# LayerNorm's sums and output projection in one pass over y, with counts from Relu, image statistics first, and fewer scan steps beside norm 0

## The chip, the core and the metric

The kernel runs on one core of one Trainium2 chip. The metric is the device time of one execution in microseconds (us), as the median of several executions. The core has TensorE (matmuls), VectorE, ScalarE and GpSimd, and a SyncE queue from which this kernel issues nearly all its transfers (DMA). Each engine works through its own instructions in order and waits for other engines and transfers by semaphores. In the profile they are PE, DVE, ACT, POOL and SP; PEld is the loading of weights into TensorE, and SPq an entry of SyncE's DMA queue.

## What is computed

Four images of 96 channels and 128x128 pixels go through two layers. The first is a state-space block on 192 channels; the second splits the result by its sign and runs an attention with 3x3 convolutions. Cut to what matters here (the group norms before each layer, weights and biases are left out; `layer_norm` stands for a mean and variance over the whole image):

```python
# layer 0, per image
z  = silu(depthwise_conv3x3(in_w @ gn(x)))               # 192 channels
for k in range(4):                                       # rows, columns, and both reversed
    h[l] = exp(delta[l] * A) * h[l-1] + delta[l] * B[l] * u[l]     # the scan, u = z in order k
    y_k  = C * h + D * u
ym = y0 + y1 + y2 + y3
yn = (ym - mean_c(ym)) * rsqrt(var_c(ym) + 1e-5) * ln_w + ln_b     # over the 192 channels of a pixel
x  = x + out_w @ yn                                      # 192 -> 96 channels

# layer 1, per image
v   = gn(x) - mean(gn(x))
x1, x2 = relu(v), v - relu(v)
pos = count(v > 0)                                       # with the sums of x1 and x1**2, both halves' statistics
x1, x2 = x1 + normed(x1), x2 + normed(x2)                # "the halves"
# attention: two convolved maps of x1 and x2 give a softmax weight per channel pair and tap,
# a third map of x1 is convolved with it; a fourth, of x2, is multiplied by x1
out = x + residual + w_full @ concat(layer_norm(attention), layer_norm(conv(x2)) * x1)
```

The scan runs over 16384 positions; the kernel cuts it into 384 steps of 1024 positions on 128 channels.

## The kernel before

The kernel is written as Python generators that emit instructions and yield a cost. `co_run(left, right, pace)` interleaves two of them: for each unit of cost that `left` has emitted, `right` emits `pace` units. `Later` holds back a function for some ticks, so that it is emitted behind other work. The emission order is then the order of each engine up to the end of image 0's maps.

The body before the loop over images, cut:

```python
last = ssm_scan(zb, xdt, xbc, yms, ready)
with tc.tile_pool(name="wp", bufs=1, side="left") as wp:
    weights = project_weights(wp)
    stats = {}
    stats[0], run = image_stats(0, wp)
    with tc.tile_pool(name="a0", bufs=4, side="left") as p2:
        drain(run(p2, 4))
    first = len(traced())
    for images, pace in (([0], 0.25), ([1], 0.75), ([2, 3], 1.35)):
        left = projections(images, weights, stats, wp, psl)
        co_run(left, last, pace)                 # input projection beside the scan
        drain(left)
four, nine = pair_weights()
...
left = imgs[0].norm(yms[0][0], psl, "left")      # "norm 0": ssm_output, then split_norm
co_run(left, last, 1.2)
drain(left)
left = direct_maps(imgs[0], psl)                 # "the maps of image 0", nine-tap convolutions
co_run(left, last, 0.75)
drain(left)
drain(last)                                      # what is left of the scan
in_order(first)
...
for b in range(NB):                              # attention of image b
    light = []
    if b:
        light.append(imgs[b - 1].close(psr, "right"))
    if b + 1 < NB:
        imgs[b + 1] = Image(b + 1)
        light.append(imgs[b + 1].norm(yms[(b + 1) // 2][(b + 1) % 2], psr, "right"))
    light = chain(*light)
    left = imgs[b].attend(psl)
    co_run(left, light, 0.5 if b else 1.5)
    drain(left)
    drain(light)
```

Image 0's maps are made ahead of the loop, so its attention there is short, and "norm 1" runs beside it.

A half of a scan step on VectorE, ScalarE and TensorE, cut:

```python
nc.tensor.matmul(pBC, lhsT=wbc[...], rhs=xr[...])        # B and C spread over channels; three banks
nc.vector.tensor_mul(p, dl, p)                           # times B
nc.vector.tensor_tensor_scan(h, h, p, init, ALU.mult, ALU.add)
nc.vector.tensor_mul(dl, dA, pC)                         # times C
# besides: softplus and exp on ScalarE, times u and the sum into y on GpSimd
```

`ssm_output`, which makes the LayerNorm and the output projection of an image in two passes over y (SN = 1024 positions, NS = 16 chunks), cut:

```python
mq = [p2.tile([128, H], F32, name=f"mq{i}", bufs=1) for i in range(2)]
ahead = load_y(0)
for c in range(NS):                                  # pass 1
    y = ahead
    if c + 1 < NS:
        ahead = load_y(c + 1)
    sq = p2.tile([C, 2, SN], F32, name="rx")
    nc.scalar.activation(sq, y, AF.Square)
    ... # 8 matmuls with mean192: means of y and y*y; copied to st, and by DMA into mq's rows
ahead = load_y(0)
later.flush()
m, q = mq
nc.vector.tensor_mul(m, m, m)                        # the whole image at once, 128 x 128
nc.vector.tensor_sub(q, q, m)
nc.vector.tensor_scalar(q, q, 0.0, None, ALU.max)
nc.scalar.activation(q, q, AF.Sqrt, bias=eps)
nc.vector.reciprocal(q, q)
rd = dram.tile([L], F32, name="rd")
nc.sync.dma_start(rd.rearrange("(p f) -> p f", f=W), q)
...
for c in range(NS):                                  # pass 2
    y, (rb, xc) = ahead, near
    if c + 1 < NS:
        ahead, near = load_y(c + 1), load_r(c + 1)   # load_r: rd spread over 96 partitions, and x
    t = p2.tile([C, SN], F32, name="xo")
    for h in range(2):
        ... # 2 matmuls po = outws.T @ y
        # held back: t = po * rb; t = t + outbs + xc; bn_stats(t); then the store to xnew
```

The counting loop of `split_norm` (the loop for the halves behind it isn't changed):

```python
for i in range(NS):
    y = ahead
    if i + 1 < NS:
        ahead = piece(i + 1)
    z = p2.tile([C, SN], F32, name="xz")
    nc.scalar.activation(z, y, AF.Identity, scale=a, bias=shift0)
    later(lambda ...: nc.vector.tensor_scalar(
        y, z, 0.0, None, ALU.is_gt, ALU.add, accum_out=cnt[:, 0, i : i + 1]))
    r = p2.tile([C, SN], F32, name="xr")
    nc.scalar.activation(r, z, AF.Relu, accum_out=cnt[:, 1, i : i + 1])
    nc.scalar.activation(r, r, AF.Square, accum_out=cnt[:, 2, i : i + 1])
```

Of the kernel before, what the change touches and what calls it, by code (L numbers as in the profile page):

```python
# [60 lines left out]
def kernel(  # L61
# [150 lines left out]

    wdt = const.tile([KS, 3, NK, 128], BF16, name="wdt", tag="wdt")
    wbc = const.tile([KS, 3, 2, 128], BF16, name="wbc", tag="wbc")
    with tc.tile_pool(name="w0", bufs=1) as w0:
        wf = w0.tile([RANK, NK, 2 * C], F32, name="wf")
        nc.gpsimd.dma_start(wf, dt_wT)
        one = w0.tile([3, 128], BF16, name="one")  # L220
        nc.vector.memset(one, 1.0)
        nc.vector.memset(wdt, 0.0)
        nc.vector.memset(wbc, 0.0)
        flat = "p k c -> p (k c)"
        pieces = split3(w0, wf.rearrange(flat), [RANK, NK * 2 * C])
        for img, ch, g, p, n in PARTS:
            row = img * KI if g == 1 else 0
            for w in range(3):
                src = pieces[w].rearrange("p (k c) -> p k c", k=NK)[:, :, ch : ch + n]
                for i in range(3):  # L230
                    at = row + w * 18 + i * RANK
                    nc.gpsimd.dma_start(wdt[at : at + RANK, g, :, p : p + n], src)
            for q in range(2):
                at = row + 54 + q
                nc.gpsimd.dma_start(wbc[at : at + 5 : 2, g, q, p : p + n], one[:, :n])

    outws = const.tile([C, 2, C], F32, name="outws", tag="outws")
    outbs = const.tile([C, 1], F32, name="outbs", tag="outbs")
    with (
        tc.tile_pool(name="w3", bufs=1) as w3,  # L240
        tc.tile_pool(name="ps0", bufs=1, space=PSUM) as ps0,
    ):
        outw = w3.tile([C, 2, C], F32, name="outw")
        nc.sync.dma_start(outw, out_wT)
        for j in range(2):
            nc.vector.tensor_scalar(
                outws[:, j], outw[:, j], lnw[:, j : j + 1], None, ALU.mult
            )
        pb = ps0.tile([C, 1], F32, name="pb")
        for j in range(2):  # L250
            nc.tensor.matmul(
                pb, lhsT=outw[:, j], rhs=lnb[:, j : j + 1], start=(j == 0), stop=(j == 1)
            )
        nc.vector.tensor_add(outbs, pb, outb)

        pw = ps0.tile([C, C], F32, name="pw")
        for j in range(2):
            nc.tensor.matmul(
                pw, lhsT=mean192, rhs=outws[:, j], start=(j == 0), stop=(j == 1)
            )  # L260
        nc.vector.tensor_sub(outws, outws, pw.unsqueeze(1).to_broadcast([C, 2, C]))
# [635 lines left out]
    def ssm_output(b, yms, xnew, stats, ps, side):  # L897

        with tc.tile_pool(name="c2", bufs=2, side=side) as p2:
            xb = x[b].rearrange("c h w -> c (h w)")
            ym = yms.rearrange("(j p) l -> p j l", j=2)
            later = Later()

            def load_y(c):
                y = p2.tile([C, 2, SN], F32, name="y")
                nc.sync.dma_start(y, ym[:, :, bass.ts(c, SN)])
                return y

            mq = [p2.tile([128, H], F32, name=f"mq{i}", bufs=1) for i in range(2)]
            ahead = load_y(0)
            for c in range(NS):
                y = ahead
                if c + 1 < NS:
                    ahead = load_y(c + 1)
                sq = p2.tile([C, 2, SN], F32, name="rx")
                nc.scalar.activation(sq, y, AF.Square)
                later.tick()
# [981 lines left out]
```

## Time and profile before

| | before |
|---|---|
| median of 3 runs | 7268.67 us (7267.92 to 7278.59) |
| span of the profiled run | 7274.5 us |
| TensorE busy | 5881.5 us, 81% |
| VectorE busy | 4795.2 us, 66% |
| GpSimd busy | 3343.3 us, 46% |
| ScalarE busy | 3086.6 us, 42% |
| moved by DMA | 1277.65 MB, 176 GB/s |
| mean granted TensorE clock | 0.88 |

The shares are averages over stages that differ. The landmarks of the stages are these: the first matmul of the input projection stands at 104.5 us and the last at 2217.7 us; the first square of norm 0 at 2292.2 us; the maps of image 0 begin at 2900.1 us; the last scan on VectorE is at 3672.6 us, and the last maps matmul at 3770.3 us; the matmuls of attention 1 begin at 4284.4 us.

In the lines of the profile, `L977 PE MATMUL bank<-y,outws` is an instruction of line 977 that writes the tile `bank` from `y` and `outws`. A view by stretches gives start and end, the length, and for each engine the busy time and, in brackets, the number of instructions; then the granted clock as a share of full speed, the busy share of the 16 DMA engines and what they moved.

### The profile page before, as it was taken

To read this page: it belongs to the slowest core of one execution; us is meant where nothing else is said; L and a number is where in the kernel's file an instruction comes from. 1 tells how busy PE (TensorE), PEld (TensorE's weight loads), DVE (VectorE), ACT (ScalarE), POOL (GpSimd) and SP (SyncE) were. 2 spreads that over 40 slices of the span, in tenths; PEclk is the share of its full clock that TensorE was granted. 3 is DMA by queue.
4 is the path that set the end of the run, shared out by engine and by line. 5 is a ranking of instruction groups with operands and counts; after the bars stand their busy time and mean duration, and the time that the engine had idled before them with its cause. 6 is when DMAs were issued, how large, how long until landed. Compare 5 with 4: busy or idle time off the path is not lost. (4 is left out here: it accounts for less than half of the span.)

```text
span 7274.5 us, 72922 instructions
## 1 busy us (share of the span) xinstructions
PE 5881.5 (81%) x22236; PEld 2380.6 (33%) x22236; DVE 4795.2 (66%) x6658; ACT 3086.6 (42%) x3734; POOL 3343.3 (46%) x2050
## 2 busy tenths in 40 slices
PE   4989978788996743899987658997889987798977
PEld 1323322222221110444442224343334343334432
DVE  2247768788895778566625667366775457776587
ACT  1347767677774466455521342305223115122102
POOL 2026657778794355557611234233443333444541
PEclk9999989988996555999988879998899998899998
DMA  4556666666766765555557766686666777665455
GB/s 116 141 142 183 185 186 182 190 188 172 208 181 165 224 168 177 160 168 154 165 142 200 203 202 182 165 216 171 208 184 169 181 196 198 200 178 145 117 149 166
DMA packets 768475, 1277.65 MB, mean 176 GB/s; under 512 B 198562, under 2 KB 507710, under 8 KB 755604
## 3 DMA queue, kind: packets, MB, share of 16 engines
q1 hardware_dynamic: 765892, 1272.71, 63.6%
q8 instruction: 179, 2.93, 0.2%
q14 instruction: 212, 1.74, 0.1%
q0 software_dynamic: 2192, 0.27, 0.1%
HBM read 908.45 MB, written 296.46 MB: 166 GB/s over the span
## 5 line engine op out<-in xcount | busy, mean ns | idle before, releaser
L1219 POOL TENSOR_TENSOR t<-y 128x768 f32<-128x768 f32 (+1 forms) x352 | 543.0, 1543 | 1957.9 <-DMA y<-vd 577.1
L597 PE MATMUL bank<-y,wp 128*128 128x512 f32 (+3 forms) x3584 | 1326.5, 627 | 70.5 <-DMA y<-y 36.6
L795 POOL TENSOR_TENSOR dl<-dl,u 128x1024 f32<-128x1024 f32 x384 | 1018.1, 2651 | 760.2 <-ACT dA L763 478.2
L828 POOL TENSOR_TENSOR y<-y,dl 128x1024 f32<-128x1024 f32 x384 | 1051.8, 2739 | 666.8 <-DVE dl L820 635.4
L1243 PE MATMUL bank<-t,wd 128*128 128x384 f32 (+2 forms) x4224 | 1158.9, 500 | 57.9 <-DVE ring L1286 20.3
L816 DVE TENSOR_TENSOR_SCAN dA<-dA,pBC 128x512 f32<-128x512 f32 x768 | 981.5, 1278 | 30.7
L1292 ACT COPY s<-bank 128x384 f32<-128x384 f32 (+2 forms) x292 | 135.9, 465 | 1871.9 <-PE bank L1254 1778.6
L820 DVE TENSOR_TENSOR dl<-dA,pBC 128x512 f32<-128x512 f32 x768 | 528.3, 688 | 508.6 <-PE pBC L772 453.0
L772 PE MATMUL pBC<-xr,wbc 60*128 60x512 bf16 (+1 forms) x1536 | 547.6, 418 | 372.3 <-DVE dA L816 318.6
L1243 PEld LDWEIGHTS bank<-t,wd 128*128 128x128 f32 (+1 forms) x4224 | 559.9, 170 | 611.3 <-issue 324.4
L1243 PE MATMUL bank<-t,wa 128*96 128x384 f32 (+1 forms) x1408 | 561.8, 548 | 235.8 <-DVE t L1220 123.2
L597 PEld LDWEIGHTS bank<-y,wp 128*128 128x128 f32 (+3 forms) x3584 | 461.4, 170 | 765.3 <-issue 678.8
L1601 PE MATMUL bank<-y,wn 128*128 128x384 f32 (+5 forms) x2408 | 653.8, 502 | 37.1 <-DMA y<-x1d 26.1
L639 ACT ACTIVATE dl<-pd,dtb 128x512 f32<-128x512 f32 x768 | 486.2, 684 | 248.1 <-PE pd L746 224.3
L1284 DVE TENSOR_TENSOR d<-s,bank 128x384 f32<-128x384 f32 (+2 forms) x292 | 156.1, 534 | 574.8 <-ACT s L1292 465.5
L799 DVE TENSOR_TENSOR pBC<-dl,pBC 128x512 f32<-128x512 f32 x768 | 527.0, 686 | 1.1
L763 ACT ACTIVATE dA<-dl,negA 128x1024 f32<-128x1024 f32 x384 | 420.2, 1141 | 2.3
L1243 PEld LDWEIGHTS bank<-t,wa 128*96 128x96 f32 x1408 | 240.7, 185 | 547.5 <-issue 407.9
L1601 PEld LDWEIGHTS bank<-y,wn 128*128 128x128 f32 (+3 forms) x2408 | 308.0, 167 | 321.6 <-issue 166.5
L639 ACT ACT_TABLE_LOAD x240 | 307.9, 1283 | 237.0 <-PE pd L746 234.0
L772 PEld LDWEIGHTS <-wbc 60*128 60x128 bf16 (+1 forms) x1536 | 113.1, 99 | 872.6 <-issue 862.1
L1220 POOL TENSOR_TENSOR t<-y 128x384 f32<-128x384 f32 (+1 forms) x352 | 368.3, 1046 | 0.0
(247 smaller groups left out, 7888.5 us busy)
## 6 DMA issues: line engine op xcount, KB each, us to landing
u<-zb SPq DMA_DIRECT2D x192, 1024.0 KB
y<-yms SPq DMA_DIRECT2D x128, 768.0 KB
xr<-xdt SPq DMA_DIRECT2D x768, 72.0 KB
yms<-y SPq DMA_DIRECT2D x96, 512.0 KB
xn<-xnew SPq DMA_DIRECT2D x128, 384.0 KB
y<-y SPq DMA_DIRECT2D x128, 258.2 KB
zb<-z SPq DMA_DIRECT2D x64, 512.0 KB
y<-vd SPq DMA_DIRECT2D x168, 193.8 KB
```

Of the source, the lines that this page charges most:

```text
L597: nc.tensor.matmul(blocks(pz[p:e]), lhsT=ws[k][:, d, c : c + e - p], rhs=window(ys[k], at, d, n), start=(i == 0), stop=(i == len(terms) - 1),)
L639: nc.scalar.activation(dst, src, AF.Softplus, bias=bias)
L763: nc.scalar.activation(live[m]["dA"], live[m]["dl"], AF.Exp, scale=negA[:, g % 3, k : k + 1])
L772: nc.tensor.matmul(p, lhsT=wbc[0 : xr.shape[0], steps[n][0] % 3, q], rhs=xr[:, at : at + CH], start=True, stop=True,)
L795: nc.gpsimd.tensor_mul(t, t, u_view(n))
L799: nc.vector.tensor_mul(p, live[n]["dl"][:, bass.ts(half, CH)], p)
L816: nc.vector.tensor_tensor_scan(h, h, p, init, ALU.mult, ALU.add)
L820: nc.vector.tensor_mul(live[n]["dl"][:, sl], live[n]["dA"][:, sl], live[n]["C", half])
L828: nc.gpsimd.tensor_add(v, v, t.rearrange("p (a b) -> p a b", b=W))
L1219: eng.tensor_sub(v[:, 0:2], of(y, 0), of(y, 2))
L1243: nc.tensor.matmul(pc[p:e, :n], lhsT=w[:, i, c : c + e - p], rhs=t[k][:, i, :n], start=(k == 0), stop=False,)
L1601: nc.tensor.matmul(pc[p:e, :n].rearrange("p (h w) -> p h w", w=W), lhsT=w[:, c : c + e - p], rhs=v[:, :, 0:W], start=(i == 0), stop=(i == ...
```

## The change

1. **One pass over y.** A chunk's squares, sums, reciprocal root, projection, scaling and store follow each other, a chunk behind. y is loaded once and the result is written over y's first half. The root is made for each chunk (8 x 128) and goes through DRAM to 96 partitions chunk by chunk. y has three buffers, the squares one.
2. **Counts from Relu.** Relu with scale and bias reads the loaded piece itself, so the Identity pass is left out; the count is taken from Relu's result, which is over 0 where the value is.
3. **Image statistics load first.** The statistics of image 0 are emitted ahead of the weights of the projection, the scan and the output, which are wrapped into functions.
4. **Paces.** The scan's pace beside norm 0 goes from 1.2 to 0.25, and beside the maps of image 0 from 0.75 to 0.95.

The aim is to read y once, to take ScalarE's third pass away, to begin the projection sooner, and to place the scan's steps beside the maps rather than beside norm 0.

```diff
@@ ssm_output (cut)
-            mq = [p2.tile([128, H], F32, name=f"mq{i}", bufs=1) for i in range(2)]
-            ahead = load_y(0)
-            for c in range(NS):
...
+            def deviations(c):
+                y = ys[c]
+                sq = p2.tile([C, 2, SN], F32, name="sq", bufs=1)
+                st = p2.tile([128, CH], F32, name="st", bufs=1)
+                mq = p2.tile([RS, 2, W], F32, name="mq")
+                m, q = mq[:, 0], mq[:, 1]
+                pm = bank(ps)
+                def sums():
...                 # the 8 matmuls as before
+                    later(lambda: nc.scalar.copy(st, pm))
+                    later(rows, 1)
+                def rows():
+                    for i in range(2):
+                        nc.sync.dma_start(mq[:, i], st[32 * i : 32 * i + 65 : 64])
+                    later(inverse, 1)
+                def inverse():
+                    nc.vector.tensor_mul(m, m, m)
+                    nc.vector.tensor_sub(q, q, m)
+                    nc.vector.tensor_scalar(q, q, 0.0, None, ALU.max)
+                    nc.scalar.activation(q, q, AF.Sqrt, bias=eps[0:RS])
+                    nc.vector.reciprocal(q, q)
+                    later(back)
+                def back():
+                    to = rd[bass.ts(c, SN)]
+                    nc.sync.dma_start(to.rearrange("(p f) -> p f", f=W), q)
+                    near[c] = p2.tile([C, 2, SN], F32, name="rx")
+                    nc.sync.dma_start(near[c][:, 1], xb[:, bass.ts(c, SN)])
+                    later(lambda: nc.sync.dma_start(near[c][:, 0], to.partition_broadcast(C)))
+                nc.scalar.activation(sq, y, AF.Square)
+                later(sums, 1)
+            load_y(0)
+            load_y(1)
+            yield 2.0
+            for c in range(NS + 1):
+                if c < NS:
+                    deviations(c)
+                later.tick()
+                yield 1.4
+                later.tick()
+                yield 1.4
+                if c:
+                    y = ys.pop(c - 1)
+                    rx = near.pop(c - 1)
+                    t = y[:, 0]
+                for h in range(2):
+                    if c:
...                     # 2 matmuls po = outws.T @ y of chunk c - 1
...                     # scaled(): t = po * rx[:, 0]; t = t + outbs + rx[:, 1]; bn_stats(t)
+                        later(scaled, 1)
+                        if h:
+                            to = xnew[:, bass.ts(c - 1, SN)]
+                            later(lambda t=t, to=to: nc.sync.dma_start(to, t), 2)
+                    later.tick()
+                    yield 1.4
+                later.tick()
+                yield 1.4
+                later.tick()
+                load_y(c + 2)
+                yield 1.4
@@ split_norm, counting loop
+                r = p2.tile([C, SN], F32, name="xr")
+                nc.scalar.activation(
+                    r, y, AF.Relu, scale=a, bias=shift0, accum_out=cnt[:, 1, i : i + 1]
+                )
+                later(lambda y=y, r=r, i=i: nc.vector.tensor_scalar(
+                    y, r, 0.0, None, ALU.is_gt, ALU.add, accum_out=cnt[:, 0, i : i + 1]
+                ))
                 z = p2.tile([C, SN], F32, name="xz")
-                nc.scalar.activation(z, y, AF.Identity, scale=a, bias=shift0)
...
-                r = p2.tile([C, SN], F32, name="xr")
-                nc.scalar.activation(r, z, AF.Relu, accum_out=cnt[:, 1, i : i + 1])
-                nc.scalar.activation(r, r, AF.Square, accum_out=cnt[:, 2, i : i + 1])
+                nc.scalar.activation(z, r, AF.Square, accum_out=cnt[:, 2, i : i + 1])
                 later.tick()
-                yield 3.5
+                yield 2.4
@@ the body
-        weights = project_weights(wp)
         stats = {}
         stats[0], run = image_stats(0, wp)
         with tc.tile_pool(name="a0", bufs=4, side="left") as p2:
             drain(run(p2, 4))
+        weights = project_weights(wp)
+        wdt, wbc = scan_weights()
+        outws, outbs = output_weights()
...
-    co_run(left, last, 1.2)
+    co_run(left, last, 0.25)
     drain(left)
     left = direct_maps(imgs[0], psl)
-    co_run(left, last, 0.75)
+    co_run(left, last, 0.95)
```

## The prediction

> **What bounds the kernel now.** I read first the busy time of each engine by stretch, with the cuts at the kernel's stages; then TensorE's order of instructions, to count the scan steps in each stage; last the timelines of the DMA queue and VectorE around norm 0, because single transfers decide there. The average (TensorE busy 81%) says little: the stages have different limits.
>
> The stretches of the kernel before (start:end, length, busy us of each engine with its instruction count, granted clock, DMA share, GB/s):
>
> ```profile
> core 0: us, PE busy (x) PEld busy (x) DVE busy (x) ACT busy (x) POOL busy (x), PEclk, DMA share, GB/s
> 0.00:105.00 105.00, 3.02 (x13) 2.65 (x14) 31.65 (x78) 6.82 (x8) 41.72 (x76) 1.00 0.37 95
> ...
> 2218.00:2290.00 72.00, 19.22 (x64) 4.67 (x62) 38.82 (x48) 20.12 (x24) 32.81 (x13) 0.55 0.50 131
> 2290.00:2400.00 110.00, 93.71 (x300) 16.32 (x301) 34.96 (x43) 63.46 (x60) 30.43 (x13) 0.55 0.77 208
> 2400.00:2625.00 225.00, 146.34 (x237) 42.77 (x237) 182.07 (x209) 88.05 (x95) 90.94 (x37) 0.62 0.77 215
> 2625.00:2740.00 115.00, 44.93 (x90) 10.32 (x91) 90.75 (x133) 104.42 (x135) 73.06 (x30) 0.50 0.54 155
> 2740.00:2900.00 160.00, 41.51 (x78) 8.33 (x77) 149.23 (x143) 109.30 (x107) 97.20 (x60) 0.50 0.56 182
> 2900.00:3675.00 775.00, 732.85 (x3011) 350.67 (x3011) 503.07 (x620) 405.87 (x537) 459.49 (x176) 0.96 0.57 162
> 3675.00:3770.00 95.00, 94.35 (x433) 54.00 (x432) 8.59 (x17) 18.72 (x35) 2.14 (x1) 1.00 0.45 110
> 3770.00:3900.00 130.00, 91.50 (x383) 26.63 (x380) 42.65 (x76) 38.58 (x38) 20.50 (x18) 0.78 0.66 165
> 3900.00:4085.00 185.00, 131.43 (x327) 51.14 (x324) 122.47 (x193) 5.97 (x11) 33.53 (x23) 0.82 0.87 234
> 4085.00:4180.00 95.00, 62.91 (x157) 23.21 (x156) 61.56 (x129) 57.09 (x88) 23.94 (x25) 0.77 0.65 175
> 4180.00:4285.00 105.00, 26.04 (x81) 13.59 (x80) 66.79 (x103) 58.74 (x54) 15.33 (x43) 0.58 0.70 218
> ...
> 5300.00:6300.00 1000.00, 860.98 (x3635) 386.96 (x3635) 639.07 (x1014) 283.18 (x362) 372.81 (x358) 0.92 0.70 189
> 6300.00:7150.00 850.00, 719.65 (x3351) 353.13 (x3350) 586.18 (x870) 147.17 (x211) 391.84 (x339) 0.93 0.54 149
> ```
>
> Norm 0 beside the scan takes 2218 to 2900: 72 us until y arrives, 110 for the sums, 225 for the projection, 115 for the counts, 160 for the two halves. No engine is full after 2625, and the clock is near half. The maps of image 0 (2900 to 3770) are the opposite: TensorE is busy 733 of 775 us and 94 of 95, and the scan, over at 3675, leaves VectorE and GpSimd empty at the end. Norm 1 (3770 to 4285) runs beside the short attention of image 0; its projection is near the DMA's limit (share 0.87, 234 GB/s). Attention 2 with norm 3 takes 1000 us, attention 3 without a norm 850, so a later norm costs about 150 us.
>
> The DMA queue in norm 0 and 1 (start, duration, engine line, out<-in):
>
> ```profile
> 2403.72 0.36 SPq L958 DMA_DIRECT2D rd<-mq  x1
> 2407.70 0.34 SPq L962 DMA_DIRECT2D rx<-rd  x1
> ...
> 2620.39 0.31 SPq L991 DMA_DIRECT2D xnew<-xo  x1
> 2623.52 0.77 SPq L1027 DMA_DIRECT2D xn<-xnew  x2
> ...
> 4080.51 0.31 SPq L991 DMA_DIRECT2D xnew<-xo  x1
> ...
> 4088.76 0.78 SPq L1027 DMA_DIRECT2D xn<-xnew  x2
> ```
>
> Each second line waits for the first to land: 4.0 us for the root written to DRAM, 3.1 us for a store of xnew in a quiet queue, 8.2 us for the same store with attention's loads ahead of it. VectorE starts on the first broadcast at 2411.49, 3.8 us after its issue.
>
> **What the skill says.** "DMA: Bandwidth & Descriptors", section "Anatomy of one DMA", puts a fixed cost near 2 us on a transfer, mostly the receipt at its end, and says that a wait for a semaphore is served by the issuing sequencer, not the DMA engine. It describes the GpSimd path; the 3.1 to 4.0 us above, on the SyncE queue, fit it, and the second point means that one waiting store holds up everything behind it. "ScalarE: Activation LUTs", "What ACT_TABLE_LOAD costs", gives 1283 ns; the load for Sqrt in norm 0 takes 1.28 us here. "TensorE: Matmul & The Clock Gate", "The HAM clock gate", says that the array runs slowly unless kept busy: 0.50 to 0.62 in norm 0 against 0.96 to 1.00 beside the maps.
>
> **The change, part by part.**
>
> *Start.* In the before the image's loads wait behind the scan's weights and start at 63.4; the first projection matmul stands at 104.5. Now the 28 us of loads start at about 11, and the weights follow. But the output weights still wait for the scan's 44 weight copies on GpSimd (17.9 to 42.3), whose source is now loaded after the projection weights, near 60. So 60 + 27 for copies + 9 for y and its shifted copies = about 97. **-6 us.**
>
> *One pass over y in norm 0.* The second load of y goes: 16 of 768 KB, 12.6 MB. The matmuls stay. What was two throughput loops becomes one loop with a cycle in it. In the new queue order the store of chunk c-1 is followed by the load of chunk c+2, which overwrites the same one of three buffers and so waits for that store to land; behind it stand the root's write and its broadcast, which waits for the write. VectorE then scales chunk c, and only then can c be stored. One turn: store 3.1 + root's write 4.0 + broadcast 3.8 + two halves of VectorE work (0.686 + 0.744 + 0.682 each, its three rows) 4.2 = 15.1; I add 2 for the y and x loads (768 and 384 KB) now queued ahead of write and broadcast. 17 us, times 16, and 18 to fill: 290 us against 335 for both loops before. Six of 25 scan steps remain in it, in its waits.
>
> *Counts from Relu.* Per piece ScalarE had 1.24 + (1.06 + 0.19) + (1.06 + 0.19) = 3.7 us, now 1.24 + 0.19 + 1.06 + 0.19 = 2.7 us. With two piece buffers the chain load 3.5, Relu 1.4, count 1.3 and a few waits gives 6.8 / 2 = 3.4 us: 16 take 55 against 115, because the scan is mostly gone too (2 steps instead of 14).
>
> *Halves.* Not changed, but 4 scan steps lie beside them instead of 13. Norm 1 did the same 16 pieces in 85 us without a scan (its ScalarE row starts from 4182.6 to 4267.5). I take 92 against 160, and 15 us for statistics between the parts. Norm 0 after its first y: 610 to about 455. **-155 us.**
>
> *The moved scan.* TensorE's order gives, of 384 steps, 243 ahead of norm 0's first sums in both kernels. Before, 52 lie within norm 0 and 89 beside the maps, over when 86% of the maps' matmuls are done; after, 13 and 128, over at 98%. So 39 steps move from where TensorE had room to where it has none. A step has 8 matmuls of 512 columns; two take 0.60 us there, so 2.4 us a step: +95 us. From rates: 285 maps matmuls per 100 us with 12 steps against 184 in 50 us without any gives 1.9 us. VectorE needs 5.3 us a step (two each of 0.69, 1.28, 0.69), and a step would come every 7.3 us: it fits. **+95 us.**
>
> *Norm 1.* The same loop with the store at 8 us instead of 3: 20 us or more a turn if nothing gives, 340 for the loop against 315 before; for it speak 12.6 MB less in a stretch at 234 GB/s (54 us). I call the loop even. Counts give 17 us (16 times 1.06). **-20 us.**
>
> *Norms 2 and 3* run at half pace beside attention. A chunk has six ticks of 1.4 at pace 0.5, so 16.8 units of attention, about 24 us, more than the turn. They lose 12.6 MB each and gain stops in the one DMA queue. **0, give or take 60.**
>
> Sum: -6 - 155 + 95 - 20 = -86; 7268.7 - 86 = **7183 us**.
>
> **Rivals.** (1) *The new cycle becomes the bound.* For it: the measured landings, 8.2 us under load, and the blocked queue that also feeds attention. If a turn is 20 us in norm 0 and 25 in norm 1, they lose 51 and 110 us, and two attentions perhaps 30 each: near 7400. Against it: a blocked queue drains, so the next landing is shorter. (2) *The bytes win.* Norm 1's loop follows its traffic and gains 55 us, the later norms 30 each, and the scan hides in TensorE's small gaps at 1.9 us: near 7050. (3) *The move pays for itself and no more.* The maps slow by over 3 us a step because TensorE, in order, waits for the scan's three spread banks (it waited on VectorE for these in norm 0): 25 to 45 us more, near 7220.
>
> **Range and chances.** The terms I trust least are the turn (3 us over 16 turns is 48 us, twice), the moved scan (30 us) and the later norms (60 us). Together about 105 us of spread: 7050 to 7320. Faster by over 2% means below 7123, which needs rival 2 in part: 0.27. Slower by over 2%, above 7414, needs rival 1 in full: 0.09. Within 2%: 0.64.
>
> **What would show it.** Right: first projection matmul near 97; norm 0 from first square to last half near 455 us; maps some 95 us longer with TensorE over 95% busy; first matmul of attention 1 about 85 us earlier. The cycle: stores of xnew in norm 0 every 17 us, with VectorE idle ahead of the scaling for the broadcast. Wrong: turns of 20 us or more; maps beyond 1000 us; the stretches of attention 1 and 2 longer than 1015 and 1000 us by over 60, with waits for maps' loads grown; or stores closer than 15 us, for then the landings overlap in a way I haven't seen.

## The result and the profile after

The changed kernel takes 7241.83 us (median of 4 runs, 7226.73 to 7251.85) against 7273.63 us of the kernel before on the same chip: the ratio is 0.9953, with a 95% interval of 0.9930 to 0.9975. The forecast was 86 us less; it came to 32 us less. In the two profiled executions the spans differ by 50 us (7274.5 and 7224.9; the execution profiled of the changed kernel lies below its median), and these 50 are what the stages below add up to.

The stretches of the changed kernel (start:end, length, busy us of PE, PEld, DVE, ACT and POOL with their instruction counts, granted clock, DMA share, GB/s), cut at its own stages:

```profile
2284.00:2585.00 301.00, 191.18 (x427) 46.13 (x427) 140.70 (x208) 83.40 (x87) 29.80 (x12) 0.62 0.48 133
2585.00:2650.00 65.00, 6.61 (x14) 1.72 (x14) 30.54 (x51) 46.99 (x72) 7.20 (x7) 0.50 0.50 142
2650.00:2760.00 110.00, 13.56 (x27) 2.93 (x28) 71.82 (x94) 75.94 (x71) 23.98 (x40) 0.50 0.66 212
2760.00:3360.00 600.00, 504.63 (x1986) 245.02 (x1987) 391.78 (x478) 331.12 (x419) 368.77 (x141) 0.91 0.57 164
3360.00:3766.00 406.00, 398.16 (x1679) 183.54 (x1677) 323.16 (x397) 248.67 (x325) 307.11 (x115) 1.00 0.60 173
3766.00:4115.00 349.00, 248.59 (x816) 87.68 (x815) 204.79 (x367) 57.23 (x71) 67.37 (x58) 0.80 0.62 168
...
4284.00:5298.00 1014.00, 844.78 (x3694) 388.14 (x3694) 710.26 (x1108) 278.13 (x367) 398.33 (x363) 0.90 0.65 178
5298.00:6298.00 1000.00, 833.17 (x3689) 384.62 (x3688) 699.55 (x1101) 274.23 (x363) 390.15 (x366) 0.92 0.65 179
6298.00:7100.00 802.00, 691.89 (x3277) 340.29 (x3275) 554.61 (x817) 141.02 (x203) 378.47 (x327) 0.95 0.55 151
```

Norm 0's loop is the first line, the counts the second, the halves the third. No engine is near full in the loop, and the DMA share is 0.48. Then the maps of image 0 fall in two: for 600 us TensorE is busy 84% of the time at a clock of 0.91, and for the last 406 us 98% at 1.00, although VectorE, GpSimd and the scan do more per microsecond there than ahead of it. That first line is the surprise of this profile.

With the ends of stages taken from the first and last instruction of each, the terms of the prediction read:

| term | forecast | measured | of it (forecast in brackets) |
|---|---|---|---|
| start and projection | -6 | -6 | first projection matmul at 101.8, not 104.5 |
| norm 0, first sum to first maps matmul | -155 | -134 | loop 294 us (290), to the first half 73 (55), halves to maps 106 (92 + 15) |
| maps of image 0 | +95 | +136 | 870.2 to 1005.9 |
| norm 1, to attention 1 | -20 | +4 | loop +30 (0), all behind it -26 (-17 in the counts) |
| attentions 1, 2, 3 | 0 | -48 | -14, -14, -20 |

The turn of the new loop is what was forecast. SyncE's queue in norm 0 of the changed kernel (start, duration, entry):

```profile
2402.83 0.32 SPq L996 DMA_DIRECT2D xnew<-y  x1
2405.93 0.32 SPq L916 DMA_DIRECT2D y<-yms  x1
2406.35 0.30 SPq L954 DMA_DIRECT2D rd<-mq  x1
...
2411.56 0.30 SPq L957 DMA_DIRECT2D rx<-rd  x1
...
2419.37 0.31 SPq L996 DMA_DIRECT2D xnew<-y  x1
```

and VectorE's first scaling of that turn:

```profile
2415.70 0.69 DVE L987 TENSOR_TENSOR y<-bank,rx 96x512 f32<-96x512 f32 x1 [4.25 <-PE bank L981]
```

Store to store takes 16.5 us: 3.1 until the store has landed and y may be loaded again, then the root's write, 5.2 until the broadcast may read it, 4.1 until VectorE scales, 3.7 to the next store. The view names TensorE as the releaser of VectorE's last wait; the broadcast lands only 0.3 us ahead of the scaling (the last update of its semaphore is at 2415.41), so the turn is a chain of transfers.

### The profile page after: what moved, and what is told of

The parts are those of the page before. It is cut to its first block, busy times and chain, and to the rows that moved or that the text cites. A ratio compares the mean times of both kernels' runs of the same rounds, so it can differ in the third digit from the quotient of the medians.

```text
span 7224.9 us, 73231 instructions
## 1 busy us (share of the span) xinstructions
PE 5742.1 (79%) x22236; PEld 2353.5 (33%) x22236; DVE 4883.6 (68%) x6898; ACT 3057.8 (42%) x3739; POOL 3342.7 (46%) x2050
## 3 DMA queue, kind: packets, MB, share of 16 engines
q0 software_dynamic: 2192, 0.27, 0.1%
## 5 line engine op out<-in xcount | busy, mean ns | idle before, releaser
L776 PE MATMUL pBC<-xr,wbc 60*128 60x512 bf16 (+1 forms) x1536 | 509.7, 398 | 280.2 <-DVE dA L820 239.3
L1612 PE MATMUL bank<-y,wn 128*128 128x384 f32 (+5 forms) x2408 | 678.8, 514 | 54.8 <-DMA y<-x1d 32.7
L1254 PE MATMUL bank<-t,wa 128*96 128x384 f32 (+1 forms) x1408 | 540.2, 531 | 227.8 <-DMA wa<-watd 73.4
L1231 POOL TENSOR_TENSOR t<-y 128x384 f32<-128x384 f32 (+1 forms) x352 | 364.1, 1034 | 0.0
L1232 POOL TENSOR_TENSOR t<-y 128x384 f32<-128x384 f32 (+1 forms) x352 | 360.4, 1024 | 0.0
```

The lines of the kernel that those rows point to most:

```text
L776: nc.tensor.matmul(p, lhsT=wbc[0 : xr.shape[0], steps[n][0] % 3, q], rhs=xr[:, at : at + CH], start=True, stop=True,)
L1254: nc.tensor.matmul(pc[p:e, :n], lhsT=w[:, i, c : c + e - p], rhs=t[k][:, i, :n], start=(k == 0), stop=False,)
L1612: nc.tensor.matmul(pc[p:e, :n].rearrange("p (h w) -> p h w", w=W), lhsT=w[:, c : c + e - p], rhs=v[:, :, 0:W], start=(i == 0), stop=(i == ...
```

## The experiments

Every run is timed against the kernel before on the same chip, so ratios are what is compared. Stage times are from one profiled execution of each kernel: norm 0 from its first square to the first maps matmul, in brackets its loop up to the last statistics; the maps of image 0; norm 1 from the last maps matmul to attention 1, in brackets its loop (in before, r2 and r17 the first chunk's sums lie beside the maps and are left out of it); and attentions 1, 2, 3.

| kernel | median us | ratio [95%] | norm 0 (loop) | maps | norm 1 (loop) | attentions |
|---|---|---|---|---|---|---|
| before | | 1 | 608 (328) | 870 | 514 (315) | 1028, 1014, 818 |
| changed | 7241.8 | 0.9953 [0.9930, 0.9975] | 474 (294) | 1006 | 518 (345) | 1014, 1000, 797 |
| r1 paces only | 7214.2 | 0.9913 [0.9889, 0.9937] | 422 (233) | 997 | 528 (319) | 1029, 1015, 814 |
| r2 old paces | 7280.3 | 1.0016 [1.0005, 1.0026] | 690 (433) | 852 | 496 (332) | 1010, 999, 798 |
| r3 rows by ScalarE | 7222.3 | 0.9933 [0.9913, 0.9953] | 475 (292) | 996 | 510 (341) | 1010, 1001, 802 |
| r4 root ahead | 7151.7 | 0.9832 [0.9813, 0.9851] | 437 (260) | 1005 | 495 (315) | 1006, 987, 797 |
| r5 rows once | 7263.2 | 0.9982 [0.9966, 0.9997] | 476 (294) | 1010 | 513 (343) | 1007, 986, 800 |
| r6 = r4 + r5 | 7194.4 | 0.9881 [0.9864, 0.9897] | 439 (261) | 1015 | 487 (311) | 996, 996, 799 |
| r7 two passes | 7207.0 | 0.9897 [0.9882, 0.9911] | 408 (233) | 1014 | 538 (313) | 1010, 1006, 808 |
| r8 u by GpSimd | 7202.5 | 0.9887 [0.9860, 0.9915] | 480 (294) | 971 | 513 (340) | 1023, 1001, 794 |
| r9 = r4 + r8 | 7130.1 | 0.9789 [0.9760, 0.9819] | 444 (260) | 982 | 494 (318) | 1007, 989, 800 |
| r10 paces, Relu | 7222.4 | 0.9917 [0.9891, 0.9944] | 412 (237) | 1017 | 538 (318) | 1014, 1006, 810 |
| r11 = r9 + rows by GpSimd | 7080.6 | 0.9745 [0.9720, 0.9771] | 442 (260) | 927 | 495 (317) | 1014, 981, 796 |
| r12 = r9, u in all steps | 7125.2 | 0.9794 [0.9772, 0.9816] | 436 (247) | 962 | 489 (313) | 1007, 996, 809 |
| r13 even rows | 7076.2 | 0.9718 [0.9698, 0.9737] | 466 (295) | 919 | 515 (342) | 1003, 1006, 803 |
| r14 even rows, once | 7073.7 | 0.9718 [0.9698, 0.9738] | 468 (296) | 909 | 515 (344) | 1006, 1007, 799 |
| r15 = r4 + r14 | 6992.3 | 0.9602 [0.9586, 0.9619] | 434 (260) | 915 | 488 (309) | 1019, 994, 799 |
| r16 = r11 + r13 | 6991.9 | 0.9601 [0.9586, 0.9616] | 434 (259) | 908 | 494 (316) | 1000, 992, 800 |
| r17 before, even rows | 7154.3 | 0.9820 [0.9804, 0.9837] | 577 (305) | 832 | 515 (315) | 1032, 1024, 812 |
| r18 = r7 + r13 | 7059.2 | 0.9689 [0.9667, 0.9710] | 398 (227) | 921 | 531 (311) | 1022, 1007, 816 |

### Which part pays: r1, r2, r7, r10

r1 is the kernel before with nothing but the new paces; r2 is the changed kernel with the old ones:

```diff
-    co_run(left, last, 1.2)      # beside norm 0
+    co_run(left, last, 0.25)
-    co_run(left, last, 0.75)     # beside the maps
+    co_run(left, last, 0.95)
```

> The kernel before with the two paces of the change alone (0.25 beside norm 0, 0.95 beside the maps). If moving the scan is a wash, norm 0 shrinks by about what the maps grow: from first square to the maps' first matmul 608 us becomes about 465, the maps' 870 us become about 1005, and the time is 7250 to 7275. If instead the paces are what gains and the one pass costs, the time is under 7225.

> The changed kernel with the old paces (1.2 and 0.75). If the 50 us gained lie in the later attentions, which the paces do not touch, and the pace is a wash, it stays within 20 us of the changed kernel (7242): norm 0 back near 610, maps near 870. If the paces carry the gain, it goes back to 7270 or above.

The paces alone gain 0.87%, more than the whole change, and the rest of the change without them costs 0.16%. r1's two loops for norm 0 take 233 us where the one-pass loop takes 294 beside as little scan. The stretch of r1's two loops:

```profile
2286.00:2520.00 234.00, 165.37 (x414) 41.22 (x414) 96.30 (x128) 58.75 (x54) 22.35 (x9) 0.67 0.79 213
```

Set it beside the first line of the changed kernel: the two passes move more bytes in less time (213 GB/s against 133). The one pass saves 12.6 MB and then waits for single transfers in turn.

r7 is the changed kernel with the old two loops put back. r10 is r1 with the counts from Relu:

```diff
 # r10 against r1
-                nc.scalar.activation(z, y, AF.Identity, scale=a, bias=shift0)
+                nc.scalar.activation(
+                    r, y, AF.Relu, scale=a, bias=shift0, accum_out=cnt[:, 1, i : i + 1])
...              # the count from r, the squares from r; yield 2.4 for 3.5
```

> The changed kernel, except that the sums and the output projection have their two loops back, each with a pass over y; the counts from Relu, the early image statistics and the new paces stay. Theory that the one pass costs more than it saves, since each turn waits for a chain of transfers in one queue: norm 0 from its first sum to its maps about 385 to 400 us instead of 474, the end 7190 to 7215 us; and if the one pass is what made the attentions shorter, they go back to 1029, 1015 and 815 us, otherwise they stay near 1014, 1000 and 797. Rival, that the one pass is what gains in norm 0: norm 0 over 474 us and the whole over 7242 us.

> The kernel before with the new paces and the counts from Relu, but with its two loops and its old order of the start: r7 without the early image statistics. Theory that the counts from Relu made the attentions shorter (r7 against r1: 1010, 1006 and 808 us against 1029, 1015 and 814): they are near 1010, 1006 and 808 us, and the counting of norm 0 is shorter than in r1 (48 us from the loop's end in r7's profile less a few); the whole about 7205 us. Rival, that the new order of the start did it by another placing of tiles and instructions: the attentions stay at 1029, 1015 and 814 us, the whole about 7214 us.

From r1 over r10 and r7 to the changed kernel the ratios are 0.9913, 0.9917, 0.9897, 0.9953. So the Relu counts and the order of the start are within what the runs resolve, and the one pass costs 0.56% (r7 to changed), some 40 us; in the profiled executions it is 65 in norm 0, less 20 in norm 1, 13 in the attentions and 8 in the maps. r7's norm 0 came out 8 us over the upper end of its expectation, with the sign as expected. In the attentions, r10's profiled execution is 16, 9 and 3 us under r1's, and r10 differs from r1 by the Relu counts alone; but its norm 1 and maps are longer by 10 and 20 us, so a gain from the counts is not shown. That attention 3, which has no norm beside it, also differs between kernels (794 to 818) is not explained by any run.

### The turn of the one-pass loop: r4

r4 makes the root of a chunk earlier (two delays of a tick less), so that its write and the broadcast fall into the wait for the store. To have the buffers free, the product and result go to rx instead of y:

```diff
-                    later(rows, 1)
+                    later(rows)
-                later(sums, 1)
+                later(sums)
-                    t = y[:, 0]
+                    t = rx[:, 1]
-                            nc.vector.tensor_mul(t[:, sl], po, rx[:, 0, sl])
+                            nc.vector.tensor_mul(rx[:, 0, sl], po, rx[:, 0, sl])
...
```

> The changed kernel with the cycle of the one pass cut: the sums and the root of a chunk one to two ticks earlier, so that root's write stands ahead of the store of the chunk before, and the result written over x's buffer instead of y's, so that the next load of y waits for TensorE and not for the store. If the turn of 16.5 us in norm 0 is this cycle, it falls to 10 to 12 us: norm 0's loop from 295 us to about 200, norm 1's from 345 to about 290, the time to about 7100 to 7150. If the turn is set by traffic or by VectorE, it stays over 15 us, and the time over 7225.

SyncE's queue in norm 0 of r4:

```profile
2411.13 0.28 SPq L954 DMA_DIRECT2D rd<-mq  x1
...
2414.56 0.30 SPq L996 DMA_DIRECT2D xnew<-rx  x1
2414.95 0.38 SPq L957 DMA_DIRECT2D rx<-rd  x1
2415.42 0.67 SPq L916 DMA_DIRECT2D y<-yms  x1
...
2429.30 0.30 SPq L996 DMA_DIRECT2D xnew<-rx  x1
```

The root's write now stands ahead of the store, the broadcast right behind it, and the load of y no longer waits for the store. Yet a turn is still 14.7 us (the store at 2414.56, the next at 2429.30): with the store's landing out of the cycle, the chain of y, sums, rows and root is next, and VectorE waits 5.6 to 6.0 us in a turn for the rows `mq<-st`. The loop fell by 34 us to 260, not to about 200; the kernel gained 1.2% against the changed one, in norm 0, norm 1 and the attentions.

### The slow steps beside the maps: r3, r5, r6, r8, r9, r11, r12

The first stretch of the maps holds scan steps 256 to 319, a group whose 128 channels belong to two images, so that a pair of steps needs eight row transfers where most groups need four. (The one other such group lies beside the projection.) From the first scan instruction of step 256 to that of step 319 a step takes 530 / 63 = 8.41 us, and in the group behind it 445 / 63 = 7.06 us. The kernel before had only the last 25 of these 64 steps beside its maps.

What TensorE waited for in the changed kernel, from 2760 to 3360 (engine, what it was to write and at which line, waited for: us in total, times, longest):

```profile
PE bank L1612 <- DMA y<-x1d: 32.7, 8, 7.6
PE pd L750 <- DMA xr<-xbc: 24.2, 6, 6.5
PE bank L1612 <- DMA y<-x2d: 15.5, 6, 4.7
PE pd L750 <- DMA xr<-xdt: 12.3, 3, 7.4
...
PE pBC L776 <- DVE dl L824: 1.5, 4, 0.4
```

Of the 103 us of its waits, 92 are for transfers, those of the maps (`x1d`, `x2d`) and those of the scan's rows (`xr`). Rival 3 of the prediction is out: in the whole stage TensorE waits 2.4 us for the scan's spread banks (`pBC`).

Why the loads come late is seen in SyncE's queue. What it waited for in the changed kernel, from 2850 to 3350:

```profile
SPq L1595 <- DMA u<-zb: 35.3, 13, 4.1
SPq L1595 <- DMA xr<-xdt: 26.2, 41, 1.2
...
SPq L1595 <- PE bank L1612: 10.4, 14, 3.9
```

Line 1595 loads the maps' own tiles, which have nothing to do with u or xr. The trace explains it: SyncE's 6114 transfers carry semaphores 108 to 115 in rotation (in r3, ScalarE's transfers carry the same eight), and each waits for its semaphore, that is, for the landing of the eighth before it. SyncE's issuing instructions take 70% of the time from 2860 to 3340 (the shares in the expectations below, 80 and 87%, include the pauses inside the timeline's merged entries); over the group's 530 us the queue further waits 107 us for landings and only 31 us for engines. So it is behind: waits for buffers (`PE bank`), which would show it ahead of its readers, are small.

r3 lets ScalarE's queue ask for the second image's rows of that group. r5 brings the three copies of the rows in one broadcast transfer, the copies outermost, with the rows laid out anew in DRAM and their stores split in two; r6 adds r4:

```diff
 # r3
+                    queue = nc.scalar if a and g == 4 else nc.sync
-                        nc.sync.dma_start(xr[at + 18 * w : at + 18 * w + 18], src)
+                        queue.dma_start(xr[at + 18 * w : at + 18 * w + 18], src)
 # r5
-                    for w in range(3):
-                        nc.sync.dma_start(xr[at + 18 * w : at + 18 * w + 18], src)
+                    nc.sync.dma_start(
+                        xr[at : at + 54], src.unsqueeze(0).to_broadcast([3, 18, 2 * SN]))
```

> The changed kernel with the row loads of the second image in scan steps 256 to 319 (four transfers a pair of steps) issued by ScalarE's queue instead of SyncE's; the bytes and their order are the same. If the maps are slow in these steps (TensorE busy 83 to 87% until 3360 us) because one queue has too many transfers to issue, TensorE is busy over 92% there, the maps shrink from 1006 us to about 965, and the time is about 7200. If TensorE is held by the scan's spread banks or the interleaving with VectorE, nothing changes: maps 1000 us or more, time 7235 to 7250.

> The changed kernel, except that the three copies of the step rows come in one broadcast transfer instead of three, so that a pair of scan steps of the group for both images asks for 4 row transfers and not 8, and of the other groups 2 and not 4. The bytes are the same. Theory that the number of transfers in SyncE's queue holds the scan of steps 256 to 319 back: TensorE over 95% busy in these steps beside the maps, the maps stage about 930 us instead of 1006, the whole about 7165 to 7190 us. Rival, that bytes, the order of the transfers or another engine hold these steps back: TensorE stays at 83 to 89% there, the maps stage 990 us or more, the whole about 7240 us.

> The changed kernel with the inverse deviations a turn earlier in the one-pass loop (as in r4, 7152 us) and the row transfers of r5. If the two gains are of different stages they add up: about 7080 to 7110 us under the theory of the number of transfers, about 7150 us under its rival.

Both missed: the maps take 996 and 1010 us. SyncE's issuing fell to 56% (r3) and 59% (r5), so fewer entries in the queue are not the remedy, and r6 loses against r4 (0.9881 for 0.9832) as r5 does against the changed kernel. The same view of r5, from 2850 to 3350, tells why:

```profile
SPq L1595 <- DMA xr<-xdt: 55.9, 27, 4.4
SPq L1595 <- DMA u<-zb: 35.7, 20, 2.9
```

What the issuing gave up, waits for landing took. r5 also lengthened the projection by 45 us, with 152 more stores of rows in it; that is more than its whole loss of 0.29% against the changed kernel.

r8 takes the largest transfers, those of u, out of the rotation, by having GpSimd ask for them in that group; r9 adds r4; r11 also takes the second image's rows out; r12 is r9 with u by GpSimd in all steps:

```diff
 # r8
+                queue = nc.gpsimd if g == 4 else nc.sync
-                    nc.sync.dma_start(u, ...)
+                    queue.dma_start(u, ...)
 # r11, on r9
+                    queue = nc.gpsimd if a and g == 4 else nc.sync
```

> The changed kernel, except that GpSimd, which reads them, asks for the u tiles of the group for both images (32 transfers, the largest loads of the scan) in place of SyncE. In the built program the transfers of SyncE and ScalarE share eight semaphores in rotation, so that each waits for the landing of the eighth before it; GpSimd's have their own. Theory that in steps 256 to 319 the loads come late because the long u transfers sit in that rotation: SyncE's waits for u<-zb (65 us in 480) go away, TensorE is over 93% busy in these steps, the maps stage takes 930 to 970 us instead of 1006, the whole 7180 to 7210 us. Rival, that the loads come late by the sum of bytes and issue times, whoever asks: the maps stage stays at 990 us or more and the whole at about 7240 us; if GpSimd loses time to the asking, more than that.

> The changed kernel with the inverse deviations a turn earlier (as in r4, 7152 us) and the u tiles asked for as in r8. If the rotation theory of r8 holds the two gains add up: about 7090 to 7120 us. If its rival holds: 7150 us or more.

> r9 (7130 us) with one part more: GpSimd asks also for the second image's step rows in the group for both images, so that SyncE asks there for no more than beside a group of one image. Theory that what is left of the lateness of steps 256 to 319 in r8 and r9 (TensorE 86 to 90% busy, SyncE's queue issuing 87%, 48 us of waits for landing row transfers) is again SyncE's rotation and issue time: TensorE over 95% busy there, the maps stage 910 to 945 us instead of 981, the whole 7070 to 7100 us. Rival, that GpSimd, with 2.4 us more to ask for in each pair of steps, or the landing itself becomes the limit: maps 975 us or more, the whole 7130 us or more.

> r9 (7130 us) with the u tiles asked for by GpSimd in all scan steps, not in those of one group alone. Theory that long transfers in SyncE's rotation hold the scan back wherever a queue of many small transfers stands behind them: the projection stage also gets shorter, by 20 to 60 us of 2192, the whole 7070 to 7110 us. Rival, that beside the projection TensorE is held by other things (DVE, GpSimd and its own weight loads): the projection stage within 15 us of before, the whole within 0.3% of r9, or longer by what GpSimd loses to the asking.

r8 takes 35 us off the maps, and r11 55 off those of r9; a step of that group then takes 7.11 us, as the later ones do. In one of r11's stretches of that group:

```profile
2960.00:3060.00 100.00, 93.68 (x400) 46.22 (x397) 77.11 (x95) 59.43 (x77) 99.74 (x64) 0.97 0.55 164
```

TensorE is at 94%, and GpSimd, which has to ask for all this, is full at 99.7%, so no more can be moved there. r12 shows the limit of reading waits: beside the projection GpSimd's waits for u fall from 126 to 32 us, and the projection is no shorter (2199 us against r9's 2192).

### What made the landing slow: r13, r14, r15, r16

A row transfer copies 18 rows of 4 KB, but in DRAM they lay as 3 pieces of 6. The Trainium skill ("DMA: Bandwidth & Descriptors", section "Why a DMA increments its semaphore by 16 and not by 1") says that a transfer goes to the largest number of DMA engines, up to 16, that divides the outermost dimension of both sides: 3 here, and 3 for r5 as well. r13 lays the same rows evenly, 18 in a row, and permutes the weights to match; the transfers are as many and as large. r14 then also brings the three copies in one, innermost:

```diff
 # r13
-            dram.tile([2, 3, n, L], BF16, ...)
+            dram.tile([2, n, 3, L], BF16, ...)
-                    src = xdt[img][k % 2, :, r : r + RANK, sl]
+                    src = xdt[img][k % 2, r : r + RANK, :, sl].rearrange("r i f -> (r i) f")
...              # xbc alike; the stores and the rows of wdt and wbc follow the order
 # r14, on r13
+                        xr[at : at + 54],
+                        src.unsqueeze(1).to_broadcast([18, 3, 2 * SN]),
```

> The changed kernel with the step rows laid out in DRAM so that the 18 rows of a transfer follow each other evenly (before: 3 pieces of 6), and the weights in the same order; as many transfers, of the same bytes. The Trainium skill (DMA: Bandwidth & Descriptors, section Why a DMA increments its semaphore by 16 and not by 1) says that a transfer goes to as many DMA engines, up to 16, as divide both sides' outermost dimension: 3 before, 9 now. Theory that slow landing of row transfers confined to few DMA engines holds steps 256 to 319 back, through the rotation of semaphores: the waits for landing row transfers shrink, TensorE is over 92% busy in these steps, the maps stage takes 930 to 970 us instead of 1006, the whole 7165 to 7205 us. Rival, that the landing of row transfers does not matter: 1000 us or more and 7235 to 7245 us.

> As r13, and the three copies of the rows in one transfer, with the copies innermost, so that it too has 18 rows outermost (in r5 the copies were outermost, so 3). Theory that r5 brought nothing because its transfers were as few but landed more slowly: SyncE issues less than 80% of the time in steps 256 to 319, TensorE is over 95% busy there, the maps stage takes 915 to 945 us, the whole 7140 to 7180 us. Rival, that the number of transfers does not matter: as r13 within 15 us.

> r14 with the inverse deviations a turn earlier in the one-pass loop (as in r4, 7152 us). If both gains hold they add up: 7060 to 7100 us. If r14 brings nothing: about 7150 us.

> r11 (7081 us: inverse deviations a turn earlier, u and the second image's rows of the group for both images asked for by GpSimd) with the row layout of r13. Theory that quick landing of rows also helps where SyncE's queue is long in other stages: 7050 to 7075 us. Rival, that r11 had already taken all that the queue held back: within 0.3% of 7081 us.

r13 is far better than its expectation: 87 us off the maps, a little more than expected, and 59 us off the projection, which no theory had counted on. What SyncE's queue of r13 waited for in the group's steps, from 2740 to 3240:

```profile
SPq L1444 <- ACT ring L1626: 39.0, 14, 5.6
SPq L1595 <- PE bank L1612: 29.6, 26, 5.1
SPq L1595 <- DMA u<-zb: 22.8, 11, 3.1
```

Waits for `xr<-xdt` are gone from the head of the list. Waits for engines lead it, for ScalarE to write what line 1444 stores and for TensorE to free a buffer: the queue is ahead again. TensorE's waits for transfers come to 30 us from 2694 to 3140, against the 92 above. Issuing got cheaper too. Two entries of the changed kernel's queue, three row transfers and the one of B and C (an entry of several includes the pauses between them):

```profile
3002.92 2.25 SPq L697 DMA_DIRECT2D xr<-xdt  x3
3005.21 0.67 SPq L700 DMA_DIRECT2D xr<-xbc  x1
```

and of r13's:

```profile
2911.25 1.10 SPq L697 DMA_DIRECT2D xr<-xdt  x3
2912.40 0.29 SPq L700 DMA_DIRECT2D xr<-xbc  x1
```

The stretch of these steps in the changed kernel, and then in r13:

```profile
2860.00:3340.00 480.00, 409.46 (x1662) 200.25 (x1661) 328.71 (x402) 267.59 (x343) 315.41 (x118) 0.92 0.57 165
```

```profile
2740.00:3140.00 400.00, 375.50 (x1606) 191.48 (x1605) 317.97 (x389) 257.46 (x331) 308.81 (x115) 0.97 0.65 190
```

Nearly the same count of work on every engine, in 400 us rather than 480, and more bytes per second (190 GB/s for 165), so bytes were not the limit. Of the 80 us, 46 are idle time of TensorE; the other 34 are busy time, at a granted clock of 0.97 for 0.92 and with 3% fewer matmuls. No run changes the clock alone. A step of the group takes 447 / 63 = 7.10 us.

The trace also shows how the rows land. From the start of its issue to the last update of its semaphore, a transfer `xr<-xdt` of this group takes 5.0 us (median) in the changed kernel and 2.9 us in r13. And each of the 768 such transfers updates its semaphore 4 times in the changed kernel and in r13 10 times: once 0.4 or 0.2 us behind the issue, then 3 or 9 times as its parts land. That is what the rule of divisors gives, 3 engines before and 9 after.

Two things changed together in r13, the landing and the issue time. r14 against r5 tells them apart, since both bring the copies in one transfer. Two entries of r5's queue, and then of r14's:

```profile
3001.64 0.75 SPq L695 DMA_DIRECT2D xr<-xdt  x1
3002.43 0.71 SPq L700 DMA_DIRECT2D xr<-xbc  x1
```

```profile
2914.64 0.82 SPq L696 DMA_DIRECT2D xr<-xdt  x1
2915.50 0.46 SPq L702 DMA_DIRECT2D xr<-xbc  x1
```

SyncE issues no less in r14 (64% of the group's time, r5 59%). But `xr<-xdt` lands after 5.3 us there, in 9 parts, and in r5 after 9.8 us, in 3; TensorE's waits for `xr` fall from 54 to 6 us, and the maps from 1010 to 909. So it is the landing that held these steps back. And r14, with a third of the row transfers, is no better than r13 (0.9718 both): their number does not matter.

The same shape is left elsewhere. Line 1213 of the changed kernel loads three copies of 32 partitions with the copies outermost, 220 times in the attentions; each updates its semaphore 4 times and lands after 9.0 to 9.3 us (medians of its three sources). No run changes these.

r15 and r16 are the fastest, 4.0% under the kernel before. r16 is no better than r15: with even rows, the help of GpSimd is not needed.

### The change without that limit: r17, r18

r17 gives the kernel before r13's rows; r18 gives them to r7.

> The kernel before with the row layout of r13 and nothing else. Theory that the moved scan was dearer than forecast because of the slow row transfers: the kernel before has 25 of the 64 steps of that group beside its maps, so it gains 30 to 40 us there (830 to 840 us instead of 870), some 59 us beside the projection as r13 did, and takes 7165 to 7190 us; the change with even rows (r13, 7076 us) is then worth 90 to 115 us, about what was forecast for it. Rival, that even rows help both kernels alike: 7100 to 7130 us, and the change is worth no more than before, 30 to 50 us.

> The changed kernel with even rows and with the two loops of the sums and the projection (r7 and r13 together). Theory that the one pass costs 35 to 40 us whatever the rows do: 7035 to 7050 us, against 7076 us of r13 with one pass. Rival, that the one pass lost because row transfers stood in its queue: 7070 us or more.

r17's maps take 832 us, 38 less than in the kernel before, as the theory said for 25 slow steps in place of 64. The whole came out 11 us under its range; norm 0, with its 52 scan steps, gained 30 us as well. r13 against r17 is the change with the limit away: 0.9718 / 0.9820 = 0.9896, or 78 us by the medians, with the moved scan at +87 us (832 to 919). That lies between the two theories' 90 to 115 and 30 to 50 us.

r18 lies between its two theories. The loops still cost what they cost (norm 0 295 us in one pass, 227 in two; norm 1 342 and 311), but the attentions are 33 us shorter with one pass (r13), so that of the 40 us about 20 are left by the ratios; as the intervals of r13 and r18 overlap, a loss is no longer shown.

## Why the prediction was off

The sign was right; the gain was a third of the forecast. By its own steps:

- **Start.** The -6 was met by luck. The first projection matmul came at 101.8 and not 97, and r1 and r10, which keep the old order, have it at 102.3 and 102.8, with norm 0's first square at 2286.2 and 2289.0 (changed: 2286.1). So no gain of the new order is shown.
- **One pass over y in norm 0.** The turn was right (16.5 us for 17), and so was the loop (294 for 290). But the step set it against two loops that carried the old pace of the scan. r1 shows what those do once the scan rests: 233 us. So the pace alone gains 95 us in the loop (328 to 233), and the one pass gave some 60 of them back.
- **Counts and halves.** The halves were right, 106 us for 107. The counts were 18 us short: the first Relu stands 7.3 us behind the loop's end, since the store before it must land, and the 16 pieces then take 62.6 us, 3.9 each for the forecast 3.4, with ScalarE waiting for the loads of pieces.
- **The moved scan: the step that failed.** +95 us was worked out from TensorE's and VectorE's time for a step, with the words "it fits". It measured +136. The steps moved are all of the group for two images, and they were limited by neither engine but by the row transfers in SyncE's queue, which landed in 3 parts after 5.0 us and through the rotation held up the loads behind them: 8.41 us a step and not 7.06. With the rows laid evenly the same move measures +87, within 8 us of the forecast. The price of a step was right; the sum lacked a term for the queue: 39 more such steps beside the maps, times 1.35 us, is 53 us, for the 41 measured over the forecast.
- **Norm 1.** "I call the loop even" was the wrong choice between two figures that stood there: the 340 us from the turn were measured as 345. That figure was luck in part: it took the store at 8 us, and in norm 1 of the changed kernel a store of xnew lands after 3.4 us (median). What grew instead are the rows `mq<-st` (6.0 us, 2.4 in norm 0) and the broadcast `rx<-rd` (5.6 us, 3.3 in norm 0). The bytes saved bought nothing, as in norm 0: the DMA share of this stretch is 0.62, where the two stretches of the kernel before had 0.66 and 0.87.
- **Norms 2 and 3.** Called 0, give or take 60; attentions 1 to 3 gained 48 us, which made up for half of what was lost elsewhere. r10 against r1 would give 28 of them to the Relu counts, and r18 against r13 33 to the one pass, but each is one execution against another, so the cause is not shown.

Of the rivals, the first was right in norm 1 (the cycle bounds the loop) and wrong for the attentions; the second, bytes, is refuted by r1; the third had the size of the maps' loss nearly right with a wrong cause.

## What to carry to other kernels

Before moving work beside an engine that is full, ask the transfer queue as well: work that "fits" by engine time can still be held up by the transfers it brings along, and the sign of it is a load that waits for the landing of an unrelated transfer. When such a transfer is slow, look at its outermost dimension on both sides before thinning out the queue: a layout in DRAM was worth 2.4% here (0.9953 to 0.9718), where asking for fewer transfers, or through other engines, had brought between a loss of 0.3% (r5) and a gain of 0.9% (r11 against r4). And fusing two passes saves bytes but may put round trips through DRAM in series; try it against the old loops at the same pace.

## What was not expected of the hardware

The same 72 KB row transfer cost SyncE 0.68 us (median) to issue as 3 pieces of 6 rows and 0.31 us as 18 rows in a row; the smaller one of 24 KB, 0.67 and 0.30 us. And a transfer that GpSimd asked for, the u tile of 1024 KB, took it 0.59 or 0.93 us by the order in which u is read (r8), little enough until four row transfers of 0.55 us more for each pair of steps filled the engine to 99.7% (r11).
